# Attention's last four heads with the queries on partitions, divided and finished 128 tokens at a time

## The chip, the cores and the metric

The kernel runs on one core of a Trainium2 chip. What counts is the device time of one execution in microseconds. Three runs of the kernel before took 2172.04, 2159.49 and 2159.13 us (median 2159.49). A further execution under the hardware profiler gave the trace that all profile lines come from.

## The reference, cut to what matters

Two blocks of a model, each with a mixing layer and a mixture of experts side by side, on 8 sequences ("batches") of 512 tokens and 256 features. The change lies at the very end of the second block's attention:

```python
def _reference_tuple_inner(x, Wq, Wk, Wv, Wo, W_down_kv, W_up_k, W_up_v):
    ...
    scores = jnp.einsum('bhqd,bhkd->bhqk', qh, kh) * scale
    ...                                       # clip, decay by distance, clip
    attn = jax.nn.softmax(scores, axis=-1)
    out = jnp.einsum('bhqk,bhkd->bhqd', attn, vh)
    out = out.transpose(0, 2, 1, 3).reshape(B, S, D_MODEL)
    return (out @ Wo, latent_kv)
...
x = x + _L1_attn_ref(...) + _L1_ffn_ref(...)   # attention plus routed experts
```

There are 16 heads of 16 features. The softmax's division may come after the product with the values: the kernel keeps unnormalised exponentials, and each head's values carry a seventeenth column of ones, so that the product brings the sum of the exponentials along.

## The kernel before, in words

Everything is float32. The attention of the second block is a sequence of 128 steps, one for each batch b (8), group g of four heads (4) and chunk c of 128 queries (4). The order on every engine is the order in which the Python text issues instructions (a manual schedule); nothing is moved later. A loop over n = 0 to 130 issues step n's scores, step n-1's exponentials and step n-2's transposes in one pass, so three steps are in work at once.

- `Step.scores`: four matmuls (L1343) give 128 queries by 512 keys for four heads, in four PSUM banks. VectorE (DVE) clips them (L1348), multiplies by the decay and takes the maximum (L1350), and negates it (`ng`, L1354).
- `Step.exps`: ScalarE (ACT) takes exp with that maximum as bias (L1358).
- `Step.transpose`: TensorE (PE) turns each head's 128x512 exponentials, 128 columns at a time (L1365), into one of two banks `p_ps`; ACT copies them to `pT` (L1366), which holds keys on partitions and two chunks of queries as columns.
- `Step.values`: every second step, for a pair of chunks, 16 matmuls (L1374) with the values as stationary operand. `o_ps`, one bank, holds the four heads at partitions 0, 32, 64 and 96: 16 rows of output and the row of sums each, queries as columns.
- `divide`: a generator for each group, in the list `chains`, of which each pass of the loop runs one part. ACT copies `o_ps` to `os` (L1384), SP stores it to the DRAM tile `od` (L1385). In the next pass, after every second group (g = 1 and g = 3), the outputs come back as 128 rows of `oT` and the sums as a 128x32 tile `sm` (L1395, L1396); then DVE takes the reciprocal (L1401), SP stores it to `rd` and reads it back spread over each head's 16 rows as `rb` (L1402, L1404), and two passes later DVE multiplies (L1407). `oT` has two halves, [:, 0, :] for heads 0 to 7 and [:, 1, :] for heads 8 to 15.
- `finish`: for each 128 tokens two matmuls with `w_o` (L1287) into the one bank `bank`, an ACT copy `fo` (L1289), and DVE's addition to `x_sb` (L1291). Then `send` stores the batch's four tiles of 128 tokens (L1299).
- `combine` runs beside it: GpSimd (POOL) gathers the two expert rows of each token (L1308), and DVE adds them to `x_sb` (L1322), seven tiles behind; the last 14 additions are issued together in the last step with scores.

After the loop, what is left of `chains` and `finish` runs to its end. SP's queue holds all stores and loads named here, in the order of issue; one that waits holds up those behind it.

Of the kernel before, what the change touches and what calls it, by code (L numbers as in the profile page):

```python
# [8 lines left out]
FP = mybir.dt.float32  # L9
I32 = mybir.dt.int32  # L10
AF = mybir.ActivationFunctionType
ALU = mybir.AluOpType
# [4 lines left out]
P = 128  # L17
B, S, DM = 8, 512, 256
NT = B * S
NTILE = NT // P  # L20
TPB = S // P
KC = DM // P
# [18 lines left out]
AH, AD, DL = 16, 16, 64  # L41
# [9 lines left out]
def bc(ap, axis, shape):  # L51

    return ap.unsqueeze(axis).to_broadcast(shape)
# [3 lines left out]
def tile_kernel(ctx: ExitStack, tc: tile.TileContext, t, out: bass.AP):  # L57
    nc = tc.nc
    V, A, G, T, Y = nc.vector, nc.scalar, nc.gpsimd, nc.tensor, nc.sync
# [4 lines left out]
    def ctile(name, shape, dtype=FP, pool=None):  # L64
        return (pool or const).tile(shape, dtype, name=name, tag=name)
# [7 lines left out]
    ident = ctile("ident", [P, P])  # L73
# [238 lines left out]
    for d in range(2):  # L312
        for q in range(2):
            r = slice(q * HP2, (q + 1) * HP2)
# [19 lines left out]
    def bank(name, shape, tag="gen"):  # L334
        return mp.tile(shape, FP, name=name, tag=("e", "s")[tag] if isinstance(tag, int) else tag, bufs=2)
# [130 lines left out]
    with ExitStack() as es:  # L466
        p1, p2, psum = m1, m2, mp
# [490 lines left out]
        N = len(chunk)  # L958
# [37 lines left out]
        with tc.manual_schedule(engines=ENGINES):  # L996
# [34 lines left out]
            def fill(n):  # L1031
                for _ in range(n):
                    if next(rows, "end") == "end":
                        next(rest, None)
# [72 lines left out]
    x_sb = res.tile([P, NTILE, DM], FP, name="x_sb", tag="x_sb")  # L1107
    with tc.tile_pool(name="a1", bufs=1) as p1, tc.tile_pool(name="a2", bufs=2) as p2, tc.tile_pool(
        name="ap", bufs=1, space=PSUM
# [127 lines left out]
        def load_some(k):  # L1237
            for to, of in loads[:k]:
                Y.dma_start(out=to, in_=of)
            del loads[:k]  # L1240

        def inputs_of(b, xT, got):
            rows = rows_qk()
            got["v"] = p2.tile([P, TPB, VW], FP, name="vt", tag="vt")
            yield from project(
                xT, lat, lambda n: p1.tile([P, KC, S], FP, name=n + "c", tag="qkc"), got["v"], rows, bank,
                lambda n: spread(rows, got, n),
            )
# [28 lines left out]
        def turn(pool, i):  # L1277
# [2 lines left out]
            V.tensor_copy(at, slot1[:, i, :])  # L1280
            return at

        def finish(b, oT):
            for c in range(TPB):
                fp = bank("fin", [P, DM])
                for j in range(KC):
                    T.matmul(fp, oT[:, j, c * P : (c + 1) * P], w_o[:, j, :], start=(j == 0), stop=(j == KC - 1))  # L1287
                fo = p2.tile([P, DM], FP, name="fo", tag="fo")
                A.copy(fo, fp)  # L1289
                xi = x_sb[:, b * TPB + c, :]  # L1290
                V.tensor_tensor(xi, xi, fo, ALU.add)  # L1291
                yield
            finished.add(b)
            if b in combined:
                send(b)

        def send(b):
            for i in range(b * TPB, (b + 1) * TPB):
                Y.dma_start(out=out[i * P : (i + 1) * P, :], in_=x_sb[:, i, :])  # L1299
# [19 lines left out]
        def add(i, yg):  # L1319
            xi = x_sb[:, i, :]  # L1320
            for k in range(2):
                V.scalar_tensor_tensor(xi, yg[k], wsel[k][:, i : i + 1], xi, ALU.mult, ALU.add)  # L1322
            b = i // TPB
            if i % TPB == TPB - 1:
                combined.add(b)
                if b in finished:
                    send(b)

# [49 lines left out]
        def divide(b, g, op, od, rd, held):  # L1380


            os = p1.tile([P, S], FP, name="os", tag="row", bufs=2)
            A.copy(os, op)  # L1384
            Y.dma_start(out=od[g].rearrange("i r s -> (i r) s"), in_=os)  # L1385
            yield
            if g % 2 == 0:
                return
            j = g // 2
            if j == 0:  # L1390
                held.append(p1.tile([P, KC, S], FP, name="oT", tag="oT"))
            oT = held[0]
            sm = p2.tile([P, 32], FP, name="sm", tag="sm")
            for gg in range(2):
                Y.dma_start(out=oT[64 * gg : 64 * gg + 64, j, :], in_=od[2 * j + gg, :, :AD, :])  # L1395
                Y.dma_start(  # L1396
                    out=sm[64 * gg : 64 * gg + 64, :],
                    in_=od[2 * j + gg, :, AD, :].rearrange("i (p f) -> i p f", f=32),
                )
            yield  # L1400
            V.reciprocal(sm, sm)  # L1401
            Y.dma_start(out=rd[8 * j : 8 * j + 8, :].rearrange("h (p f) -> (h p) f", f=32), in_=sm)  # L1402
            rb = p1.tile([P, S], FP, name="rb", tag="row", bufs=2)
            Y.dma_start(out=rb, in_=bc(rd[8 * j : 8 * j + 8, :], 1, [8, AD, S]))  # L1404
            yield
            yield
            V.tensor_tensor(oT[:, j, :], oT[:, j, :], rb, ALU.mult)  # L1407
            yield
            if g == 3:
                urgent.insert(0, finish(b, oT))  # L1410
# [4 lines left out]
        with tc.manual_schedule(engines=ENGINES):  # L1415
# [3 lines left out]
            finished, combined = set(), set()  # L1419
            urgent, idle, chains = [], [], []  # L1420
# [26 lines left out]
            def more():  # L1447
                if ready is not None and n > ready + 3:
                    next(rows, None)
# [19 lines left out]
            N = len(steps)  # L1469
            last_rows(1)  # L1470
            done = []
            pT, op, pair = {}, {}, None
            inputs = {0: got}
            for n in range(N + 3):

                if n < N:
                    b, g, c = steps[n]
                    if (g, c) == (0, 3) and b + 1 < B:
                        xT = p2.tile([P, KC, S], FP, name="xT", tag="xT")
                        Y.dma_start(out=xT, in_=xtd1[b + 1])  # L1480
                    if (g, c) == (1, 2) and b + 1 < B:
                        inputs[b + 1] = {"q": [], "k": []}
                        urgent.append(inputs_of(b + 1, xT, inputs[b + 1]))
                    if (g, c) == (0, 0):
                        od = dram.tile([4, 4, 32, S], FP, name="od", tag="od", bufs=2)
                        rd = dram.tile([AH, S], FP, name="rd", tag="rd", bufs=2)
                        scratch = (od, rd, [])
                    now = Step(b, g, c, inputs[b])
                    now.scratch = scratch
                    done.append(now)  # L1490
                    now.scores()
                load_some(6)
                for chain in list(chains):
                    if next(chain, "end") == "end":
                        chains.remove(chain)
                if ready is not None and n == ready + 3:
                    idle.append(work)
                begun = n >= 1
                if begun:
                    fill()  # L1500
                if 1 <= n <= N:
                    done[n - 1].exps((0, 1))
                m = n - 2
                if m >= 0 and m % 2 == 0 and m >= 2:

                    s = done[m - 1]
                    if s.c == 1:
                        s_op = psum.tile([P, S], FP, name="o_ps", tag="o_ps", bufs=1)
                    s.values(s_pT, s_op)
                    if s.c == TPB - 1:  # L1510
                        chains.append(divide(s.b, s.g, s_op, *s.scratch))
                        next(chains[-1])
                    if begun:
                        fill()
                if 0 <= m < N:
                    if m % 2 == 0:
                        s_pT = [p2.tile([P, TPB, 2 * P], FP, name="pT", tag="pT", bufs=5) for _ in range(4)]
                    done[m].transpose(s_pT, (0, 1))
                if begun:
                    fill() or more()  # L1520
                if 1 <= n <= N:
                    done[n - 1].exps((2,))
                if 0 <= m < N:
                    done[m].transpose(s_pT, (2,))
                    if m % 2 == 1 and n < N // 2:
                        fill()
                    done[m].transpose(s_pT, (3,))
                if begun:
                    fill() or more()
                if 1 <= n <= N:  # L1530
                    done[n - 1].exps((3,))
                follow()
# [80 lines left out]
```

## Time and profile before

| | |
|---|---|
| median of three runs | 2159.49 us (2159.13 to 2172.04) |
| the profiled execution's own time | 2153.93 us |
| its span in the trace | 2152.2 us |
| mean granted TensorE clock | 0.929 |
| PE, DVE, ACT, POOL busy | 1874.2, 1463.6, 1187.6, 636.4 us |
| last maxima of the scores done on DVE | 2117.07 us |
| last group's values end on PE | 2125.9 us |
| last group's product with the reciprocals begins on DVE | 2138.87 us |
| last addition to `x_sb` | 2148.88 us, 0.42 us long |

Times in the trace are microseconds from the start of the span. A line of an engine's timeline gives the start, the duration of the run of equal instructions, the engine, the source line, the operation with its output and inputs, their sizes, how many, and in brackets the idle time before it and what ended it. A float32 matmul of the program shows as two records on PE. PEld is the loading of the stationary operand, SPq is SP's queue. In a line of the windows stand the stretch and its length, the busy time and number of instructions of PE, PEld, DVE, ACT and POOL, then the granted TensorE clock (1.00 is full speed), the share of the DMA engines, and GB/s.

### The profile page before, as it was taken

How to read it: one execution, taken by the hardware profiler on the slowest of the kernel's cores; microseconds unless marked ns; L12 is line 12 of the kernel's file. 1: busy time of each engine (PE TensorE's matmuls, PEld its weight loads, DVE VectorE, ACT ScalarE, POOL GpSimd, SP SyncE). 2: the span in 40 equal slices, each digit the busy share in tenths (PEclk: the TensorE clock that was granted, in tenths of full speed). 3: DMA queues.
4: the chain of work that ended last, by engine and by line, in shares of the span. 5: the costliest groups of instructions: out<-in, count | busy, mean ns of one | idle time of the engine just before them, and what ended most of it. 6: DMA issues, size and time to landing. Idle time of an engine off the chain costs nothing. (4 is left out here: it accounts for less than half of the span.)

```text
span 2152.2 us, 33599 instructions
## 1 busy us (share of the span) xinstructions
PE 1874.2 (87%) x11792; PEld 1240.4 (58%) x11792; DVE 1463.6 (68%) x3328; ACT 1187.6 (55%) x2562; POOL 636.4 (30%) x592
## 2 busy tenths in 40 slices
PE   5649999999999999987867778999999999999785
PEld 5325666766766676644544444656666666666343
DVE  5745666767584666577648896766666676767795
ACT  2235453545444354545426676767677777777563
POOL 0075453646363454445410253000000000000452
PEclk9879999999999999988887788999999999999787
DMA  7134454646463464444523342121121212121354
GB/s 257 56 103 169 152 191 146 222 142 221 140 203 138 135 230 134 142 135 127 162 94 112 96 144 89 63 103 61 65 81 60 97 63 82 62 77 54 89 109 94
DMA packets 156361, 263.69 MB, mean 123 GB/s; under 512 B 25018, under 2 KB 112622, under 8 KB 144290
## 3 DMA queue, kind: packets, MB, share of 16 engines
q1 hardware_dynamic: 124544, 144.70, 21.2%
q0 software_dynamic: 22320, 107.55, 15.3%
q10 hardware_dynamic: 9330, 9.31, 1.3%
q8 instruction: 93, 1.52, 0.3%
q14 instruction: 74, 0.61, 0.1%
HBM read 193.44 MB, written 72.75 MB: 124 GB/s over the span
## 5 line engine op out<-in xcount | busy, mean ns | idle before, releaser
L1348 DVE TENSOR_SCALAR s<-s_ps 128x512 f32<-128x512 f32 x512 | 317.7, 683 | 235.8 <-PE s_ps L1343 185.9
L1358 ACT ACTIVATE s<-s,ng 128x512 f32<-128x512 f32 x512 | 354.2, 726 | 29.0 <-DVE ng L1354 22.2
L1365 PE MATMUL p_ps<-ident,s 128*128 128x128 f32 x2048 | 297.3, 289 | 71.0 <-ACT pT L1366 60.2
L1365 PEld LDWEIGHTS p_ps<-ident,s 128*128 128x128 f32 x2048 | 244.3, 147 | 155.9 <-ACT pT L1366 94.2
L1366 ACT COPY pT<-p_ps 128x512 f32<-128x512 f32 x512 | 278.9, 590 | 88.5 <-PE p_ps L1365 63.9
L1350 DVE CUSTOM_DVE_ANT_0 s<-s,band 128x512 f32<-128x512 f32 x512 | 322.5, 685 | 0.0
L1308 POOL DMA_INDIRECT yg<-yd,at x64 | 67.6, 1057 | 710.6 <-PE s_ps L1343 650.7
L688 PE MATMUL pj<-xT,w_in 128*128 128x512 f32 x384 | 197.5, 640 | 12.3 <-DVE cv L701 9.5
L1343 PE MATMUL s_ps<-kT,qT 16*128 16x512 f32 x1024 | 174.7, 698 | 17.5 <-DVE s L1348 10.9
L507 PEld LDWEIGHTS h_ps<-xdT,w 128*128 128x128 f32 x1248 | 153.9, 197 | 32.9 <-issue 19.0
L507 PE MATMUL h_ps<-xdT,w 128*128 128x128 f32 x1248 | 158.8, 282 | 10.3 <-ACT xdT L497 10.3
L864 POOL TENSOR_TENSOR au<-da,half 128x512 f32<-128x512 f32 x64 | 75.1, 1174 | 258.0 <-PE seg L879 162.4
L701 DVE SCALAR_TENSOR_TENSOR cv<-pj,w_conv_w,cv 128x511 f32<-128x511 f32 (+2 forms) x192 | 143.0, 746 | 9.8 <-issue 5.6
L520 PE MATMUL y_ps<-w,hT 128*128 128x256 f32 x624 | 148.2, 380 | 0.0
L1374 PE MATMUL o_ps<-pT,vt 128*32 128x256 f32 x2048 | 139.6, 415 | 0.0
L520 PEld LDWEIGHTS y_ps<-w,hT 128*128 128x128 f32 x624 | 115.9, 191 | 34.8 <-issue 19.4
L937 POOL TENSOR_TENSOR yT<-yT,ex 128x512 f32<-128x512 f32 (+1 forms) x48 | 59.9, 1248 | 255.7 <-DVE ex L936 193.6
L1200 PE MATMUL e_hp<-e_xdT,e_w 128*128 128x256 f32 x448 | 121.7, 394 | 3.0 <-ACT e_xdT L1194 2.0
L688 PEld LDWEIGHTS pj<-xT,w_in 128*128 128x128 f32 x384 | 70.6, 201 | 91.9 <-issue 82.5
L926 DVE TENSOR_TENSOR yT<-yT,yd 128x512 f32<-128x512 f32 (+1 forms) x64 | 43.8, 684 | 116.4 <-PE yd L917 114.3
L1213 PE MATMUL e_yp<-e_w,e_hT 128*128 128x256 f32 x448 | 120.0, 390 | 0.2
L1374 PEld LDWEIGHTS o_ps<-pT,vt 128*32 128x32 f32 x2048 | 64.5, 118 | 80.0 <-issue 51.1
(275 smaller groups left out, 3133.1 us busy)
## 6 DMA issues: line engine op xcount, KB each, us to landing
ex<-exd SPq DMA_DIRECT2D x96, 128.0 KB
u<-in_u_dram SPq DMA_DIRECT2D x16, 512.0 KB
xtd<-xT SPq DMA_DIRECT2D x16, 512.0 KB
fr<-fdd SPq DMA_DIRECT2D x64, 128.0 KB
od<-os SPq DMA_DIRECT2D x32, 256.0 KB
xT<-xtd SPq DMA_DIRECT2D x15, 512.0 KB
e_w<-in_ei_dram SPq DMA_DIRECT2D x7, 1024.0 KB
e_w<-in_eo_dram SPq DMA_DIRECT2D x7, 1024.0 KB
```

The costliest lines, as they stand in the source:

```text
L507: T.matmul(hp[:, i, :], w1[:, k * FF + f * P : k * FF + (f + 1) * P], xdT[:, k * P : (k + 1) * P], start=(k == 0), stop=(k == KC - 1),)
L520: T.matmul(yp, hT[f // 4][:, f % 4, :], w2[:, f * DM : (f + 1) * DM], start=(f == 0), stop=(f == FC - 1))
L688: T.matmul(pj, w_in[:, k, o * P : (o + 1) * P], self.xT[:, k, :], start=(k == 0), stop=(k == KC - 1))
L701: V.scalar_tensor_tensor(cv[:, s:], pj[:, : S - s], conv_w[:, q, 3 - s : 4 - s], cv[:, s:], ALU.mult, ALU.add)
L1200: T.matmul(hp, w1[:, k, f * P : (f + 1) * P], xdT[:, k, :], start=(k == 0), stop=(k == KC - 1))
L1343: T.matmul(sp[i], self.q[r, cols], self.k[r, :], start=True, stop=True)
L1348: V.tensor_scalar(self.p[i], sp[i], -CLAMP, CLAMP, ALU.max, ALU.min)
L1350: V.tensor_tensor_reduce(out=self.p[i], in0=self.p[i], in1=band[:, at : at + S], scale=1.0, scalar=-3.0e38, op0=ALU.mult, op1=ALU.max, acc ...
L1358: A.activation(self.p[i], self.p[i], AF.Exp, bias=self.ng[:, i : i + 1])
L1365: T.transpose(pp[:, k, :], self.p[i][:, k * P : (k + 1) * P], ident)
L1366: A.copy(pT[i][:, :, cc * P : (cc + 1) * P], pp)
L1374: T.matmul(op[32 * i : 32 * i + 32, half * 2 * P : (half + 1) * 2 * P], self.v[:, k, h * (AD + 1) : h * (AD + 1) + 32], pT[i][:, k, :], st ...
```

## The change

Only batch 7 and its last group (heads 12 to 15) are affected. There, in place of `values` for pairs of chunks, each chunk gets a generator `last_group` as soon as its transposes are done: 16 matmuls with 128 queries of `pT` as stationary operand and 17 columns of values as moving operand give queries on partitions; DVE takes the reciprocal of the four columns of sums and multiplies. In the next pass a matmul with the identity turns the 128x64 result into partitions 64 to 127, and ACT copies it into `oT`'s upper half. Then, once heads 8 to 11 are divided, two matmuls with `w_o` follow, DVE adds their result from PSUM to `x_sb`, and the tile is sent by itself. `o_q` and `t_q` use the one bank of `o_ps`.

Heads 8 to 11 (g = 2) can no longer wait for g = 3: `divide` treats them alone (`ending`), on 64 rows, and tells `last_group` by a second entry in `held`.

```diff
+        def last_group(s, held):
+            op = psum.tile([P, 4, AD + 1], FP, name="o_q", tag="o_ps", bufs=1)
+            cols = slice(s.c % 2 * P, (s.c % 2 + 1) * P)
+            for i in range(4):
+                h = 4 * s.g + i
+                for k in range(TPB):
+                    T.matmul(
+                        op[:, i, :], s.pT[i][:, k, cols], s.v[:, k, h * (AD + 1) : (h + 1) * (AD + 1)],
+                        start=(k == 0), stop=(k == TPB - 1),
+                    )
+            sm = p2.tile([P, 4], FP, name="smq", tag="smq")
+            V.reciprocal(sm, op[:, :, AD])
+            oq = p2.tile([P, 4, AD], FP, name="oq", tag="oq")
+            V.tensor_tensor(oq, op[:, :, :AD], bc(sm, 2, [P, 4, AD]), ALU.mult)
+            yield
+            oT = held[0]
+            qs = slice(s.c * P, (s.c + 1) * P)
+            tp = psum.tile([P, P], FP, name="t_q", tag="o_ps", bufs=1)
+            T.matmul(tp[64:, :], oq.rearrange("p i d -> p (i d)"), ident, start=True, stop=True)
+            A.copy(oT[64:, 1, qs], tp[64:, :])
+            yield
+            while not held[1:]:
+                yield
+            fp = bank("fin", [P, DM])
+            for j in range(KC):
+                T.matmul(fp, oT[:, j, qs], w_o[:, j, :], start=(j == 0), stop=(j == KC - 1))
+            i = s.b * TPB + s.c
+            V.tensor_tensor(x_sb[:, i, :], x_sb[:, i, :], fp, ALU.add)
+            last_sent.add(s.c)
+            if s.b in combined:
+                send_tile(i)
...
@@ add
                 if b in finished:
                     send(b)
+                elif b == B - 1:
+                    for c in last_sent:
+                        send_tile(b * TPB + c)
...
@@ divide
-            if g % 2 == 0:
+            ending = b == B - 1 and g == 2
+            if g % 2 == 0 and not ending:
                 return
...
-            for gg in range(2):
+            r, nh = (slice(0, 64), 4) if ending else (slice(0, P), 8)
+            for gg in range(nh // 4):
                 Y.dma_start(out=oT[64 * gg : 64 * gg + 64, j, :], in_=od[2 * j + gg, :, :AD, :])
...
-            V.tensor_tensor(oT[:, j, :], oT[:, j, :], rb, ALU.mult)
+            V.tensor_tensor(oT[r, j, :], oT[r, j, :], rb[r], ALU.mult)
+            if ending:
+                held.append(True)
...
@@ the loop over n
-                if m >= 0 and m % 2 == 0 and m >= 2:
+                if m > N - TPB:
+                    chains.append(last_group(done[m - 1], done[m - 1].scratch[2]))
+                    next(chains[-1])
+                elif m >= 0 and m % 2 == 0 and m >= 2:
...
+                    done[m].pT = s_pT
```

In the changed program the instructions of every engine stand in the same order as before up to the scores of the very last step; from there on they differ. On SP the loads of heads 8 to 11 stand between batch 5's and batch 6's stores, and their `rd` and `rb` behind batch 6's.

More of the change, by code (lines that the diff above doesn't have):

```diff
@@ L1281, in turn, with send_tile @@
             return at
+        def last_group(s, held):
[29 more added lines that the diff above has]
+                send_tile(i)
+        last_sent = set()
+        def send_tile(i):
+            Y.dma_start(out=out[i * P : (i + 1) * P, :], in_=x_sb[:, i, :])
         def finish(b, oT):
@@ L1400, in divide @@
             yield
-            V.reciprocal(sm, sm)
-            Y.dma_start(out=rd[8 * j : 8 * j + 8, :].rearrange("h (p f) -> (h p) f", f=32), in_=sm)
+            V.reciprocal(sm[r], sm[r])
+            Y.dma_start(out=rd[8 * j : 8 * j + nh, :].rearrange("h (p f) -> (h p) f", f=32), in_=sm[r])
             rb = p1.tile([P, S], FP, name="rb", tag="row", bufs=2)
-            Y.dma_start(out=rb, in_=bc(rd[8 * j : 8 * j + 8, :], 1, [8, AD, S]))
+            Y.dma_start(out=rb[r], in_=bc(rd[8 * j : 8 * j + nh, :], 1, [nh, AD, S]))
             yield
             yield
-            V.tensor_tensor(oT[:, j, :], oT[:, j, :], rb, ALU.mult)
+            V.tensor_tensor(oT[r, j, :], oT[r, j, :], rb[r], ALU.mult)
+            if ending:
+                held.append(True)
             yield
```

## The prediction

> **What bounds the kernel now.** I read the page, then the chain of waits that ended last, then each engine's timeline from 2085 us on, because the change touches nothing earlier: engine by engine, both kernels issue the same instructions up to the last four heads of batch 7. Chunk c below is that group's 128 queries c = 0 to 3. The end of the chain, with its columns start us, us, what:
>
> ```profile
> 2122.13 1.14 PE p_ps L1365 x8
> 2123.27 2.61 PE o_ps L1374 x32
> ...
> 2126.51 2.00 DMA od<-os
> ...
> 2129.08 4.11 DMA sm<-od
> ...
> 2135.09 3.66 DMA rb<-rd
> ...
> 2146.37 2.09 PE fin L1287 x4
> ...
> 2148.88 0.42 DVE x_sb L1291
> ```
>
> After the last transposes and values come 13 us of copies through DRAM in which the engines hardly work, then four output products one after the other, the last three at some 2.09 us. The same four records at 2055 us, in PE's timeline:
>
> ```profile
> 2055.68 1.03 PE L1287 MATMUL fin<-w_w_o,oT 128*128 128x256 f32 x4
> ...
> 2062.50 1.93 PE L1374 MATMUL o_ps<-pT,vt 128*32 128x256 f32 x32
> ```
>
> The windows say why; the column after the engines is the granted clock. It goes to 0.50 at 2129, after the wait began, and stays there while fin runs. So the end is a chain of latencies at half clock, and before 2117.1 DVE sets the pace (it ends chunk 3's maxima at 2117.07 and has no gap before).
>
> ```profile
> 2126.00:2128.00 2.00, 0.49 (x2) 0.09 (x1) 0.00 (x0) 0.49 (x1) 0.00 (x0) 1.00 0.33 124
> 2128.00:2130.00 2.00, 0.00 (x0) 0.00 (x0) 0.00 (x0) 0.00 (x0) 0.00 (x0) 0.74 0.23 68
> 2140.00:2142.00 2.00, 1.54 (x4) 0.73 (x4) 0.43 (x1) 0.37 (x1) 0.00 (x0) 0.50 0.00 0
> ```
>
> **What goes.** For this group: two values() calls (32 records each, 2.91 us at 2114.01 and 2.66 us at 2123.20), the os copy, od store, four loads, reciprocal, rd and rb, and four fo copies on ACT. The round trip through DRAM does not vanish: heads 8 to 11 still make it, one step earlier and with half the rows.
>
> **What comes.** For each chunk: 16 small matmuls (Q0 to Q3), two small DVE operations, one turning matmul (R0 to R3), one ACT copy, then fin (F0 to F3). PE's new order is: scores of chunk 3, Q0, transposes of chunk 1, R0, Q1, transposes of 2, R1, Q2, transposes of 3, F0, F1, R2, Q3, F2, R3, F3. Q and R share the single o_ps bank, so Q of the next chunk waits until ACT has copied R.
>
> The price of Q decides. The nearest row has the same full 128x128 stationary operand and few moving columns: 8 at line 603, 24 at line 148, where Q moves 17.
>
> ```profile
> 69.08 3.67 PE L148 MATMUL pp<-w_w_small,xT 128*128 128x24 f32 x16 [0.51 <-ACT xT L144]
> ...
> 959.21 1.85 PE L603 MATMUL pp<-w_w_r,xT 128*128 128x8 f32 x16
> ...
> 1061.12 3.65 PE L603 MATMUL pp<-w_w_r,xT 128*128 128x8 f32 x16 [0.18 <-ACT xT L597]
> ```
>
> The program's 8 matmuls are 16 records, so Q is 32 records. Full clock: (1.85 - 0.25 for the last) / 15 = 0.107 us apart, and 31 x 0.107 + 0.25 = 3.57 us. Half clock: (3.65 - 0.38) / 15 = 0.218, so 7.14 us. Three times as many columns (line 148) change nothing, so the weight loads set it. Bounds per Q at full clock: 1.93 us from line 1374 above (weights of 32 columns) and 31 x 0.121 + 0.29 = 4.0 us from line 1365 (1.14 us for 8, 128 columns moving). I take line 603, the nearest.
>
> The other rows: the 128x4 reciprocal 0.17 (L165), the 128x64 product 0.22 (between 0.187 for 128x32 at L608 and 0.257 for 128x96 at L152), together 0.39; R 0.4 (two 128x128 records, 0.39 at L900, 0.64 at half clock); the 64x128 ACT copy 0.3 (0.37 for 128x256 at L1289); transposes of two heads 1.1 (half clock 1.94 to 2.18); pT copies 1.06 a pair; exponentials 0.65 each; fin 1.05, or 2.07; its addition 0.42; handovers 0.05.
>
> **The sum at full clock**, from 2117.07, which both kernels share. Q0 runs 2110.4 to 2113.9 under DVE's maxima and costs nothing there; it and chunk 1's transposes push ACT to 2117.9, eating the 1.53 us that ACT waited at 2117.1. Without DVE's cover Q0 would add its 3.57. DVE's 0.39 stands ahead of the 14 additions of expert rows (6.50 us). R0 ends 2117.95 and the copy 2118.25. Behind it on ACT wait chunk 3's exponentials (1.15 us late), behind R0 on PE wait Q1 and chunk 2's transposes, which feed ACT in turn. Q1 ends 2121.85. Chunk 2's transposes and copies and chunk 3's last exponential end on ACT at 2125.85. DVE has done its additions at 2123.96, the reciprocal of heads 8 to 11 at 2124.3, chunk 1's division at 2124.7; R1 is ready, its copy ends 2126.15. Q2 ends 2129.75, chunk 3's transposes 2132.05.
>
> Heads 8 to 11: SP now issues their loads after batch 5's four stores and ahead of batch 6's (before, all eight stood together, 2107.45 to 2120.17). Batch 5's last addition is at 2110.9, so the loads land near 2116.5, before DVE asks. rd stands behind batch 6's stores, whose last addition is at 2120.3, also done by 2124.3. From the reciprocal's end to the product took 2133.64 to 2138.87, 5.23 us; here it gives 2129.55, and DVE's product ends 2130.85. This lies 1.2 us under chunk 3's transposes.
>
> F0 ends 2133.1, its addition 2133.55, F1 2134.65, R2 2135.05, copy 2135.4, Q3 2138.95, F2 2140.0, R3 2140.4, copy 2140.7. F3's first half waits for F2's addition (one bank) and it ends 2141.5, addition 2141.95. From the last addition to the end of the span, 2149.30 to 2152.2, are 2.9 us: 2144.85, or 7.3 us less than 2152.2.
>
> **But the clock.** A full clock has to survive the Qs. Line 603 ran from 1044.93 to 1046.66 (14 records), begun at full clock; the windows there:
>
> ```profile
> 1045.00:1046.00 1.00, 1.00 (x10) 1.00 (x10) 1.00 (x1) 0.00 (x0) 0.00 (x0) 1.00 0.30 123
> 1046.00:1047.00 1.00, 1.00 (x8) 0.87 (x10) 0.40 (x3) 0.00 (x0) 0.00 (x0) 0.98 1.08 352
> 1047.00:1048.00 1.00, 1.00 (x4) 0.00 (x0) 0.93 (x4) 0.00 (x0) 0.00 (x0) 0.50 0.85 226
> ```
>
> PE was recorded busy through 1045 to 1047 and the clock fell all the same. The records at 1061 and 69 us ran at half and did not raise it either. Steady transposes do: 16 records from 1155.37 at half clock, and at 1159.6 it is full. Falls and rises at 2084.6, 2091.4, 2098.2, 2105.1 and 2129.0 stand apart by multiples of about 3.4 us. A Q lasts about as long as one such interval, so I expect Q1, Q2 and Q3 at half clock and the transposes and fins mostly at full. Each Q then costs 3.57 more, all in series: 3 x 3.57 = 10.7, so 2155.55, or 3.4 us more than before. **This is the forecast**: the profiled execution took 2153.93 us with a span of 2152.2, the median of the runs shown is 2159.49, and I put the difference on the median: 2162.9.
>
> [...]
>
> **Rivals.** *The clock holds* (2152.2, 7.3 us faster). For it: between 2105 and 2128 the clock is 1.00 with PE busy some 60 to 100%, and records at 959 us ended at full. Against it: 1047 us, and a Q is twice as long as those.
>
> *All of it at half clock* (slower). Place: from about 2118, when PE has waited for R0. Working on from Q1 at 2118.25 with 7.14 per Q, 4.05 for a chunk's transposes, 2.07 per fin and 0.65 per R: Q1 2125.4, ACT free 2130.6, Q2 2138.05, transposes 2142.1, F0 2144.2, F1 2146.7, Q3 2154.85, F2 2156.9, F3 2159.6, addition 2160.05, end 2162.95. That is 10.8 us slower, 2170.3. It decides if no interval after 2118 is filled well enough to raise the clock; for it speaks that fin at 2140 to 2150 never did. With the upper bound for Q at half clock (8.0), 2.6 more.
>
> *The round trip decides* (Q near its lower bound, 1.93). F0 then waits for DVE's product near 2130.1, and the rest with a short Q3 ends 2140.65: 11.5 us faster, 2148.0. Against it: no row with 128-column weights is that quick.
>
> *The change does not shorten the chain*, because heads 8 to 11 come late: the loads would have to land after 2124, 8 us later than worked out, and chunk 1's division would stand behind them on DVE at a microsecond per microsecond. The od store is issued at 2107.08 and took 2.00 us in the chain, so I see no cause.
>
> **How the numbers follow.** Qs at half and the rest at full 0.45; clock holds 0.25; all at half 0.2; round trip 0.05; something else 0.05. No case reaches 1% (21.6 us, about what a measurement of this kernel can tell from no change), so nearly all the chance is on no change. The forecast's own range is one Q either way at the other clock, 2159.3 to 2166.5. The whole range runs from the full-clock sum on the profiled execution's own time (2153.93 - 7.3 = 2146.6) to the all-half sum with a dear Q on the median, 2172.
>
> **What would show it.** Right: 32-record rows of o_q near 7.1 us for Q1 to Q3 and 3.6 for Q0; granted clock 0.50 in windows inside the Qs; chain through o_q, t_q, oT and fin without DMA after the last transposes; a last addition near 2152. Rows of o_q at 3.6 throughout mean that the clock held; fin at 2.07 after 2132 means all at half. A DMA rb or sm row at the end of the chain, or any change before 2110, would make the reasoning wrong.

## The result, and the profile after

The changed kernel takes 2165.43 us, the median of 20 runs (2153.08 to 2174.64); the kernel before, beside it, 2161.53 us (20 runs, 2152.76 to 2173.29). The ratio, which goes by the means and not by the medians, is 1.001 with a 95% interval of 0.9992 to 1.0028: +2.2 us, between -1.7 and +6.0. That is no change, as forecast; the forecast's +3.4 us is a ratio of 1.0016, inside the interval.

The profiled execution has a span of 2160.2 us against 2152.2, 8.0 us more. 5.6 of these lie ahead of the tail: chunk 3's maxima end on DVE at 2122.67 here and at 2117.07 before, and both kernels issue the same instructions in the same order up to there on DVE, on PE up to the last scores. Over the twelve traces of this study of which this holds, this end lay anywhere from 2107.7 to 2128.6. So I read every trace from there. The **tail**, from the end of the last maxima to the end of the span, is 35.13 us before and 37.53 after.

PE's timeline of the tail, as before:

```profile
2113.48 3.75 PE L1291 MATMUL o_q<-vt,pT 128*128 128x17 f32 x32
2117.07 3.65 PE L1407 MATMUL p_ps<-ident,s 128*128 128x128 f32 x16
2123.06 0.43 PE L1303 MATMUL t_q<-ident,oq 128*64 128x128 f32 x2 [2.34 <-DVE oq L1298]
2123.84 6.90 PE L1291 MATMUL o_q<-vt,pT 128*128 128x17 f32 x32 [0.35 <-ACT oT L1304]
2130.58 3.79 PE L1407 MATMUL p_ps<-ident,s 128*128 128x128 f32 x16
2134.30 0.43 PE L1303 MATMUL t_q<-ident,oq 128*64 128x128 f32 x2
2136.01 5.54 PE L1291 MATMUL o_q<-vt,pT 128*128 128x17 f32 x32 [1.27 <-ACT oT L1304]
2141.38 3.49 PE L1407 MATMUL p_ps<-ident,s 128*128 128x128 f32 x16
2144.71 1.03 PE L1310 MATMUL fin<-w_w_o,oT 128*128 128x256 f32 x4
2146.25 1.13 PE L1310 MATMUL fin<-w_w_o,oT 128*128 128x256 f32 x4 [0.52 <-DVE x_sb L1312]
...
2148.09 4.11 PE L1291 MATMUL o_q<-vt,pT 128*128 128x17 f32 x32 [0.35 <-ACT oT L1304]
2152.04 2.05 PE L1310 MATMUL fin<-w_w_o,oT 128*128 128x256 f32 x4
2154.03 0.69 PE L1303 MATMUL t_q<-ident,oq 128*64 128x128 f32 x2
2154.65 2.08 PE L1310 MATMUL fin<-w_w_o,oT 128*128 128x256 f32 x4
```

Where the kernel before had 13 us of copies through DRAM, PE now has work nearly all the time, and none of it is quick. The four Qs are the rows of o_q: 3.75, 6.90, 5.54 and 4.11 us. The windows over them (window, its length, busy us of PE, PEld, DVE, ACT, POOL, then the granted clock, third from the end):

```profile
2116.00:2118.00 2.00, 2.00 (x16) 2.00 (x17) 1.93 (x7) 0.39 (x1) 1.00 (x1) 0.79 0.88 110
...
2136.00:2138.00 2.00, 1.99 (x17) 1.99 (x17) 0.00 (x0) 0.00 (x0) 0.00 (x0) 0.91 0.00 0
2138.00:2140.00 2.00, 2.00 (x11) 2.00 (x11) 0.00 (x0) 0.00 (x0) 0.00 (x0) 0.50 0.00 0
...
2146.00:2148.00 2.00, 1.49 (x6) 0.87 (x6) 0.62 (x2) 0.22 (x1) 0.00 (x0) 1.00 0.20 66
...
2152.00:2154.00 2.00, 2.00 (x5) 1.20 (x5) 0.41 (x2) 0.00 (x0) 0.00 (x0) 0.50 0.00 0
```

Windows of 1 us put the falls near 2117.2, 2124.0, 2137.7 and 2151.3, one in or just before each Q, and the rises near 2120.6, 2134.2 and 2144.5: neighbours stand about 3.4, 6.8 or 10.2 us apart. At 2117 and 2151 the 3.4 us before the fall hold nothing but Q0 and Q3, with PE recorded busy all along (but for 0.2 us of waiting at 2148). The fall at 2137.7 comes after R1, 1.27 us of waiting and 1.7 us of Q2 (17 records in 2136 to 2138, then 11), and the one at 2124 after a wait, R0's 2.34 us for DVE (PE was busy for 0.72 us of the 3.4 before it). The chunk's transposes that follow a Q begin at half, and under each of them the clock rises again (near 2120.6, 2134.2 and 2144.5). The end of the chain (start us, us, what) has no DMA row from 2117 on, and from the end of the maxima at 2122.67 on it runs through PE but for small steps of ACT and DVE, 0.62 us at most:

```profile
2136.01 5.54 PE o_q L1291 x32
2141.55 3.33 PE p_ps L1407 x16
2144.87 0.88 PE fin L1310 x4
...
2148.09 4.11 PE o_q L1291 x32
2152.20 1.89 PE fin L1310 x4
...
2154.72 2.02 PE fin L1310 x4
```

### The profile page after: what moved, and what is told of

The parts are those of the page before. It is cut to its first block, busy times and chain, and to the rows that moved or that the text cites. A ratio compares the mean times of both kernels' runs of the same rounds, so it can differ in the third digit from the quotient of the medians.

```text
span 2160.2 us, 33744 instructions
## 1 busy us (share of the span) xinstructions
PE 1896.2 (88%) x11864; PEld 1262.0 (58%) x11864; DVE 1464.5 (68%) x3336; ACT 1187.8 (55%) x2561; POOL 637.7 (30%) x592
## 5 line engine op out<-in xcount | busy, mean ns | idle before, releaser
L1407 PE MATMUL p_ps<-ident,s 128*128 128x128 f32 x2048 | 305.9, 295 | 63.9 <-ACT pT L1408 46.4
L1407 PEld LDWEIGHTS p_ps<-ident,s 128*128 128x128 f32 x2048 | 252.5, 151 | 149.9 <-ACT pT L1408 74.9
L1416 PE MATMUL o_ps<-pT,vt 128*32 128x256 f32 x1984 | 132.8, 413 | 0.0
L892 ACT ACTIVATE mt<-seg,mid 64x64 f32<-64x64 f32 x512 | 109.5, 308 | 0.8
```

Source lines behind the costliest of these rows:

```text
L1407: T.transpose(pp[:, k, :], self.p[i][:, k * P : (k + 1) * P], ident)
L1416: T.matmul(op[32 * i : 32 * i + 32, half * 2 * P : (half + 1) * 2 * P], self.v[:, k, h * (AD + 1) : h * (AD + 1) + 32], pT[i][:, k, :], st ...
```

## The experiments

The theory: the changed kernel's tail is a chain on PE, and its length is set by the clock, which falls in the Qs because records with 17 moving columns do not count as work for it. Rivals: the clock falls because of the waits around the Qs (PE idle 0.35 to 2.34 us before R and Q, since o_q and t_q share a bank); or the Qs are slow for another reason, such as their weight loads, whatever the clock; or the clock has nothing to do with the moving columns, and any back-to-back stream holds it. Full clock for the same chain was worked out in the prediction as a tail of 27.8 us (2144.85 - 2117.07).

**q128: Qs with 128 moving columns.** The same 32 records and weights, 111 more columns that nobody uses.

```diff
-            op = psum.tile([P, 4, AD + 1], FP, name="o_q", tag="o_ps", bufs=1)
+            op = psum.tile([P, 4, 128], FP, name="o_q", tag="o_ps", bufs=1)
...
-                        op[:, i, :], s.pT[i][:, k, cols], s.v[:, k, h * (AD + 1) : (h + 1) * (AD + 1)],
+                        op[:, i, :], s.pT[i][:, k, cols], s.v[:, k, h * (AD + 1) - 95 : h * (AD + 1) - 95 + 128],
...
-            V.reciprocal(sm, op[:, :, AD])
+            V.reciprocal(sm, op[:, :, 95 + AD])
...
-            V.tensor_tensor(oq, op[:, :, :AD], bc(sm, 2, [P, 4, AD]), ALU.mult)
+            V.tensor_tensor(oq, op[:, :, 95 : 95 + AD], bc(sm, 2, [P, 4, AD]), ALU.mult)
```

> Only the moving operand of the small matmuls is widened from 17 to 128 columns of the values (the other 111 columns are computed and not used). The tail is counted from the end of the last maxima on DVE to the end of the span: 35.1 us before, 37.5 us after. Theory (a stream of narrow matmuls lets the clock fall, though PE's records are back to back): wider ones hold it at 1.00, each group of 32 records takes about 4.0 us (31 x 0.121 + 0.29) in place of 6.90, 5.54 and 4.11, fins take 1.05, and the tail is the full-clock sum 27.8 + 3 x 0.43 = 29.1 us, some 8 us shorter than after. Rival (PE's waits for DVE and ACT let it fall): the clock falls just the same, the groups take 4 to 8 us and the tail is 37.5 us or more.

Measured: the tail is 31.60 us, between the theory's 29.1 and the rival's 37.5. Over 12 runs the median is 2150.23 against 2155.81 before beside it, the ratio 0.9993 (0.9969 to 1.0017). So more arithmetic makes the tail 5.9 us shorter than the changed kernel's 37.53, and the whole is still not measurably different from before. Q2 took 5.35 us. PE's timeline, Q1 with what is ahead of it, then Q3, and two windows:

```profile
2115.99 0.68 PE L1303 MATMUL t_q<-ident,oq 128*64 128x128 f32 x2 [1.34 <-DVE oq L1298]
2117.03 4.98 PE L1291 MATMUL o_q<-vt,pT 128*128 128x128 f32 x32 [0.35 <-ACT oT L1304]
...
2137.31 3.84 PE L1291 MATMUL o_q<-vt,pT 128*128 128x128 f32 x32 [0.35 <-ACT oT L1304]
```

```profile
2117.00:2119.00 2.00, 1.97 (x9) 1.98 (x10) 1.93 (x5) 1.33 (x2) 0.00 (x0) 0.50 0.95 90
2119.00:2121.00 2.00, 2.00 (x18) 2.00 (x18) 1.89 (x6) 0.00 (x0) 0.00 (x0) 0.89 0.90 106
```

At full clock 128 columns cost as much as 17 (3.84 against 3.75 us), so the moving columns are not what a Q's time goes into. The theory alone does not stand, though: the clock still fell twice, near 2116.0 and 2126.3, when in the 3.4 us before PE had been busy for 1.35 and 1.59 us only (waits of 1.34 and 1.38 us for DVE ahead of R, and shorter ones between the transposes). What differs is that it rose again inside the Q, near 2119.5, when of the 3.4 us before 2.4 were Q1, 0.68 R0 and the rest a wait. (The clock also rises within a Q of 17 columns, at 2130 in own_bank_2 below, but there after 3.4 us that were nearly all transposes and R0.) Waits and thin records both let it fall.

**q68: 68 moving columns**, the same edit with 51 for 95 and 68 for 128.

> The same with 68 columns. The weight loads (0.107 us apart) still set the pace at full clock, so a group costs 3.6 us if the clock holds; the columns stream for about half of the time that they do with 128. Theory: a tail between 27.8 us (the clock holds) and 37.5 us (it falls as with 17), which tells how wide is wide enough; I expect it nearer to 28 to 32. Rival (PE's waits): 37.5 us, as with 17 columns.

Measured: tail 35.76 us, a miss (28 to 32 was expected), one run of 2159.35 beside 2155.81. Q0 is 5.64 us, Q1 5.89; Q2, and Q3 with F2 behind it:

```profile
2133.88 6.41 PE L1291 MATMUL o_q<-vt,pT 128*128 128x68 f32 x32 [1.47 <-ACT oT L1304]
...
2147.62 3.79 PE L1291 MATMUL o_q<-vt,pT 128*128 128x68 f32 x32 [0.35 <-ACT oT L1304]
2151.25 1.08 PE L1310 MATMUL fin<-w_w_o,oT 128*128 128x256 f32 x4
```

The windows give the clock 0.66 in 2134 to 2136 and 0.50 from there to 2144, past Q2's end at 2140.3. So half the columns of q128 did not bring it back in Q2, and Q3 began and ended at full. Q3 did that with 17 columns in other traces too (own_bank, after_3 below), but there the clock fell right behind it: F2 took 1.65 to 2.05 us in all five traces with 17 columns, and here 1.08 us, with the windows at 1.00 from 2146 to 2152. In this one trace 68 columns did not raise a fallen clock, yet they held a full one through Q3; the tail is nearer to that with 17 than to that with 128.

**own_bank: t_q in a bank of its own**, so that Q does not wait for ACT's copy of R.

```diff
-            tp = psum.tile([P, P], FP, name="t_q", tag="o_ps", bufs=1)
-            T.matmul(tp[64:, :], oq.rearrange("p i d -> p (i d)"), ident, start=True, stop=True)
-            A.copy(oT[64:, 1, qs], tp[64:, :])
+            tp = psum.tile([P, S], FP, name="t_q", tag="s_ps", bufs=4)
+            T.matmul(tp[64:, :P], oq.rearrange("p i d -> p (i d)"), ident, start=True, stop=True)
+            A.copy(oT[64:, 1, qs], tp[64:, :P])
```

> The turned result t_q goes to a bank of the scores, free by then, so the next chunk's small matmuls no longer wait until ACT has copied it. Theory (the clock is what was lost): only the idle time of PE ahead of the three groups goes, 0.35 + 1.27 + 0.35 = 2.0 us, so a tail of about 35.5 us, give or take 2 for where the clock's intervals fall; the groups still take 4 to 7 us. Rival (the one bank shared by o_q and t_q is what was lost): most of the 9.7 us above the full-clock sum come back, a tail near 28 us.

Measured: tail 32.78 us, a miss (less than expected), one run of 2143.96 beside 2155.81. Q1 and Q2 in PE's timeline, with no idle time noted before them; Q3 took 3.75:

```profile
2110.08 6.48 PE L1291 MATMUL o_q<-vt,pT 128*128 128x17 f32 x32
...
2120.74 3.91 PE L1291 MATMUL o_q<-vt,pT 128*128 128x17 f32 x32
```

The waits gone are worth 0.35 + 1.27 + 0.35 = 1.97 us; the rest of the 4.75 us against the changed kernel is clock. The edit does not touch the Qs, and yet Q1 to Q3 take 14.14 us instead of 16.55, F2 and F3 3.58 instead of 4.13. Whether that follows from the edit or from luck was the next question.

**own_bank_2, after_2, after_3: the same kernels again.**

> The bank of its own for the turned result with 17 columns, once more: its tail was 32.8 us where 35.5 was expected, with two groups at 3.9 and 3.75 us. Theory: 2 us are the waits taken out, the rest was where the intervals fell, so now a tail of 31 to 37 us with other groups slow. Rival (the shared bank is worth nearly 5 us of itself): 32 to 33 us again with the same groups fast.

> The changed kernel once more, for how far its tail of 37.5 us goes from one execution to the next. Theory: the clock's intervals of some 3.4 us fall elsewhere against the groups each time, so each group lies between 3.6 and 7 us and the tail between 33 and 39 us; Q0 at full clock or fallen within, at least two of the four groups at over 4.5 us.

> The same a third time: a tail between 33 and 39 us, and at least two of the four groups at over 4.5 us.

Measured, one run each (2165.03, 2161.4 and 2149.18 us, beside 2153.46 before):

| trace | Q0 | Q1 | Q2 | Q3 | tail |
|---|---|---|---|---|---|
| after | 3.75 | 6.90 | 5.54 | 4.11 | 37.53 |
| after_2 | 3.79 | 7.01 | 5.66 | 4.23 | 37.65 |
| after_3 | 6.59 | 4.87 | 4.77 | 3.75 | 36.07 |
| own_bank | 3.75 | 6.48 | 3.91 | 3.75 | 32.78 |
| own_bank_2 | 6.45 | 3.90 | 4.44 | 5.74 | 34.48 |

From PE's timeline of after_3, Q0, then Q3 with F2:

```profile
2102.04 6.59 PE L1291 MATMUL o_q<-vt,pT 128*128 128x17 f32 x32
...
2136.05 3.75 PE L1291 MATMUL o_q<-vt,pT 128*128 128x17 f32 x32 [0.35 <-ACT oT L1304]
2139.64 1.65 PE L1310 MATMUL fin<-w_w_o,oT 128*128 128x256 f32 x4
```

All three tails lie where they were expected, and own_bank_2 does not repeat own_bank's fast groups. The same program can give each Q another time: it depends on where the falls and rises of the clock happen to lie against it (in after the clock fell near the end of Q0, in after_3 near 2102.5, 0.5 us after its start). One pair of traces is therefore good to a few microseconds only. The changed kernel's tail is 36.1 to 37.7, mean 37.1; own_bank's mean 33.6, some 3.5 us less, of which 1.97 are the waits. The rest (1.5 us on two traces) I would not build on.

**before_warm and before_warm2: the kernel before with PE kept busy.** During its copies through DRAM, 12 tiles (25 in the second) of four transposes whose result nobody reads.

```diff
@@ ahead of the last fill() in the kernel before
+            for _ in range(25):
+                warm = psum.tile([P, TPB, P], FP, name="warm", tag="p_ps", bufs=2)
+                for k in range(TPB):
+                    T.transpose(warm[:, k, :], ident, ident)
```

> The kernel before with 48 transposes of the identity on PE after the last values, some 11.6 us that lie in the wait for the copies through DRAM; their results are not used. Theory: the granted clock stays at 1.00, fin takes 1.05 us in place of 2.09, and the tail of 35.1 us shrinks by about 3.6 us to 31.5. Rival (fin is slow at the end for another reason, such as its single bank): 35.1 us.

> As before_warm, but with 100 transposes: there each took one record and not two, so 48 of them filled only 5.5 us and the clock fell before fin came. 100 last about 11.6 us, to some 1 us ahead of fin. Theory: granted clock 1.00 until fin, fin at 1.05 us, tail 35.1 - 3.6 = 31.5 us. Rival: fin slow for another reason, 35 us.

The first missed its purpose, because I had sized it wrongly: a transpose is one record and not two, as a matmul is. Its tail is 36.02 us (2153.47 beside 2155.81), the second's 31.64 (2141.07 beside 2151.76). The rows of the filler and the second output product, first of before_warm:

```profile
2124.50 5.46 PE L1536 MATMUL warm<-ident 128*128 128x128 f32 x48
...
2140.86 2.07 PE L1287 MATMUL fin<-w_w_o,oT 128*128 128x256 f32 x4 [0.46 <-ACT fo L1289]
```

Then of before_warm2, whose granted clock is 1.00 in every window from 2116 to 2132:

```profile
2116.38 11.14 PE L1536 MATMUL warm<-ident 128*128 128x128 f32 x100
...
2131.25 1.13 PE L1287 MATMUL fin<-w_w_o,oT 128*128 128x256 f32 x4 [0.46 <-ACT fo L1289]
```

With 11 us of filler the clock lives to the end and fin takes 1.13 instead of 2.07 us; the tail is 3.5 us shorter than before's 35.13, as expected. With 5.5 us it falls near 2134, before fin. With nothing but the filler changed this gives the price of the clock in that tail, and shows that transposes hold it; it is one trace of each.

**before_thin: the same place, Q-like records instead.** 8 tiles of four matmuls with 17 moving columns.

```diff
+            for _ in range(8):
+                thin = psum.tile([P, TPB, P], FP, name="thin", tag="p_ps", bufs=2)
+                for k in range(TPB):
+                    T.matmul(thin[:, k, : AD + 1], s_pT[0][:, k, :P], done[-1].v[:, k, : AD + 1], start=True, stop=True)
```

> The same place filled with 32 matmuls as the change has them, full 128x128 weights and 17 moving columns (64 records, nothing waits between them, results not used). Theory (narrow ones do not count as work for the clock): PE is recorded busy without a gap, yet the clock goes to 0.50 within 3.4 to 7 us of their start, and the records' distance doubles from 0.107 to 0.218 us, so that they last 8 to 12 us and not 6.9. Rival (only waits let it fall): 1.00 throughout, 6.9 us.

Measured: tail 34.89 us, one run of 2153.64 beside 2151.76. PE's timeline and the windows; fin takes 2.07 us after it:

```profile
2125.73 11.24 PE L1536 MATMUL thin<-vt,pT 128*128 128x17 f32 x64
```

```profile
2125.00:2127.00 2.00, 2.00 (x22) 1.48 (x14) 0.00 (x0) 0.58 (x1) 0.00 (x0) 1.00 0.00 0
2127.00:2129.00 2.00, 2.00 (x19) 2.00 (x18) 0.00 (x0) 0.00 (x0) 0.00 (x0) 0.90 0.46 146
2129.00:2131.00 2.00, 2.00 (x11) 2.00 (x11) 0.00 (x0) 0.00 (x0) 0.00 (x0) 0.50 0.25 76
```

64 records without a gap, with PE recorded busy for 2.00 of 2.00 us, and the clock falls from 1.00 to 0.50 about 3 us after their start and stays. At full clock they would have taken 64 x 0.107 = 6.9 us. No wait plays a part. This shows the step that decided the forecast: records with so few moving columns do not hold the clock, though PE is recorded busy. The rival that any back-to-back stream holds it falls.

**q128_own: both edits, wide Qs and t_q in its own bank.**

> The changed kernel with both edits, 128 moving columns and a bank of its own for the turned result. With 128 columns the clock still fell twice, each time after PE had waited 1.4 + 0.35 us for DVE and for the copy. Theory (both the narrow streams and the waits between them let it fall): with both gone or shortened the groups take 3.8 to 4.5 us and the tail comes to 28 to 31 us. Rival (it falls on where the intervals lie, and neither edit matters): 31 to 37 us.

Measured: tail 26.45 us, less than the 28 to 31 expected, one run of 2137.3 beside 2151.76. All four Qs took 3.84 us, and the granted clock is 1.00 from Q0 to F3. Q2:

```profile
2116.68 3.84 PE L1291 MATMUL o_q<-vt,pT 128*128 128x128 f32 x32
```

Without thin records and without the waits for the bank the clock holds (PE's longest wait from Q0 on is 1.20 us, within chunk 1's transposes), and the full-clock sum of the prediction comes near: 27.8 us. Cut at the ends of R0, Q1, Q2, F0, Q3 and the last addition, six of its seven stretches come within 0.25 us; the one from Q1's to Q2's end took 6.87 us instead of 7.90, and in it lay the wait for the bank that this kernel does not have. It is one trace; the rival, by which only the place of the clock's intervals matters, expected 31 us or more. By this trace, thin records and the waits were what stood between the changed kernel and the gain at full clock.

**turn_all: another way to the same end.** The kernel before, with heads 8 to 15 kept out of DRAM without turning the product round: `values` stays as it was (32 stationary columns, 256 moving), its result is copied to SBUF, 128x128 transposes bring queries onto partitions, DVE divides by columns, and matmuls with the identity turn it back. The fins alternate between two banks, and DVE adds straight from PSUM.

```diff
+        def turned(os, cols, tag):
+            tp = psum.tile([P, TPB, P], FP, name="t_" + tag, ...)
+            for k, c in enumerate(cols):
+                T.transpose(tp[:, k, :], os[:, c * P : (c + 1) * P], ident)
...
+            for k in range(n):
+                V.reciprocal(sm[:, k, :], t4[:, k, :, AD])
+                V.tensor_tensor(
+                    oq[:, k, :].rearrange("p (i d) -> p i d", d=AD), t4[:, k, :, :AD],
+                    bc(sm[:, k, :], 2, [P, 4, AD]), ALU.mult,
+                )
...
+        def into(oT, oq, cols, r):
+            tq = psum.tile([P, S], FP, name="t_o", tag="s_ps", bufs=4)
+            for k, c in enumerate(cols):
+                T.matmul(tq[r, k * P : (k + 1) * P], oq[:, k, :], ident, start=True, stop=True)
+            A.copy(oT[r, 1, cols[0] * P : (cols[-1] + 1) * P], tq[r, : len(cols) * P])
...
+            for c in range(TPB):
+                fp = psum.tile([P, DM], FP, name="fin", tag="p_ps", bufs=2)
...
+                V.tensor_tensor(x_sb[:, i, :], x_sb[:, i, :], fp, ALU.add)
```

> A kernel of its own, from the one before: the last group's values stay as they were (weights of 32 columns), but the output is turned on PE to 128 queries on partitions (one transpose for a chunk), divided by columns, turned back with a matmul, and the fins run in two banks with one store each; heads 8 to 11 of batch 7 go the same way, so no copy through DRAM is left after them. Theory (narrow matmuls with 128 weight columns were what cost, the idea of dividing by columns was sound): no group of 3.6 to 7 us is left, values end some 7 us after the last maxima, then 10 us of short steps and 2.9 us to the end of the span: a tail of 19 to 23 us against 35.1 before and 37.5 after, 12 to 16 us or 0.6 to 0.75% faster than before. Rival (a chain of short steps loses as much in handovers and at half clock): 30 us or more, no difference in the runs.

Measured: tail 18.50 us, just under the 19 to 23 expected; 2134.69 us median of 9 runs against 2151.76 (14 runs) beside it, ratio 0.9928 (0.9903 to 0.9954). That is 0.7% faster than the kernel before, clear of the noise, and its interval lies wholly below the changed kernel's. Several things changed at once here, so no single one of them has a price from this run. PE's timeline of its end, and a window:

```profile
2116.35 1.93 PE L1374 MATMUL o_last<-pT,vt 128*32 128x256 f32 x32
2118.21 1.00 PE L1385 MATMUL t_g<-ident,os 128*128 128x128 f32 x4
2119.28 1.38 PE L1401 MATMUL t_o<-ident,oq 128*64 128x128 f32 x8
2120.59 3.72 PE L1592 MATMUL fin<-w_w_o,oT 128*128 128x256 f32 x16
```

```profile
2121.00:2123.00 2.00, 2.00 (x11) 1.76 (x10) 0.80 (x2) 0.06 (x1) 0.00 (x0) 1.00 0.00 0
```

The product for two chunks takes 1.93 us here, where two Qs take 7.5 at full clock. The clock is 1.00 to the end, and the 16 records of the four output products take 3.72 us.

## Why the prediction was right

The forecast was no change, by a full-clock gain of 7.3 us that the clock takes back with 10.7. The measured +2.2 us (-1.7 to +6.0), and the tails of 37.1 after against 35.3 before (means of three traces each, that of the kernel before over its own, before_warm and before_thin, whose fillers did not change fin's time), +1.7, say the same; +3.4 was forecast. That the verdict is no change says little by itself, since the prediction's own cases, from 11.5 us faster to 10.8 us slower, all lie under its 1%. The interval says more: it leaves out the rivals at -11.5, -7.3 and +10.8 us. The rival in which the clock holds (27.8 us of tail) is refuted by the traces, and q128_own shows what would have made it true. In the all-half rival F0 and F1 take 2.07 us; they take 1.03 and 1.13. The round trip does not decide: DVE's timeline has heads 8 to 11 ready before F0 starts at 2144.71.

```profile
2122.57 0.17 DVE L1296 RECIPROCAL smq<-o_q 128x4 f32<-128x4 f32 x1
2122.78 0.22 DVE L1298 TENSOR_TENSOR oq<-o_q,smq 128x64 f32<-128x64 f32 x1
...
2129.34 0.34 DVE L1445 RECIPROCAL sm<-sm 64x32 f32<-64x32 f32 x1
2130.78 0.18 DVE L1296 RECIPROCAL smq<-o_q 128x4 f32<-128x4 f32 x1 [1.11 <-PE o_q L1291]
...
2141.94 0.67 DVE L1451 TENSOR_TENSOR oT<-oT,rb 64x512 f32<-64x512 f32 x1
```

They also show the loads of heads 8 to 11 hidden, since L1445 waits for nothing, and chunk 1's division waiting for PE rather than for DVE. The durations of 0.17 and 0.22 are the ones the prediction took, and R's 0.43 on PE is close to its 0.4; a Q at full clock took 3.75 us, 0.18 more than its 3.57.

The sum, stretch by stretch from the end of the last maxima:

| stretch | forecast | measured |
|---|---|---|
| to R0's end | 0.88 | 0.82 |
| to Q1's end | 7.47 | 7.25 |
| to Q2's end | 11.47 | 10.81 |
| to F0's end | 3.35 | 4.19 |
| to Q3's end | 9.42 | 6.46 |
| to the last addition's end | 3.00 | 4.98 |
| to the end of the span | 2.90 | 3.02 |

It ends within 1 us, 38.5 against 37.5, partly by **errors that cancel**. The step that failed is "Q1, Q2 and Q3 at half clock and the transposes and fins mostly at full". The clock follows with a lag (the transposes behind Q1 begin at 2130.58, and it rises near 2134.2): Q1, Q2 and Q3 took 6.90, 5.54 and 4.11 us (16.55) in place of 21.4, since Q2 and Q3 begin at the full clock that the transposes before them raised (Q1 had 0.2 us of it); in return the transposes behind Q1 and Q2 run at half for a while (3.79 and 3.49 us instead of about 2.2), and F2 and F3 take 2.05 and 2.08 in place of 1.05. Half clock thus fell on other instructions than I gave it to, in about the right amount: 22.5 us from the last maxima to F3's end, where three Qs at 7.14 make 21.4. That the amounts agree is partly luck, as the traces differ. The clock also fell at the end of Q0 (near 2117), which cost nothing, as forecast for Q0 as a whole: R0 waited 2.34 us for DVE afterwards. In after_3, where nearly all of Q0 ran at half (6.59 us), R0 had no such wait, so that cover is used up there.

A second term was missing as a cause: the waits. The forecast blamed the thin records alone; only its all-half rival let the clock fall at PE's wait for R0. There it did fall, at 2124, ahead of nearly all of Q1; q128 falls after waits of 1.34 and 1.38 us, and in q128_own, with wide Qs and no wait over 1.20 us, no fall is left.

Two workings of the prediction are off, and neither moves the forecast. It took the records at 69 us for half clock; that follows from their spacing alone, since the windows there read 1.00. What it drew from them, that more columns cost no time, q128 shows directly (3.84 against 3.75 us). And by its own terms the round-trip rival ends near 2141.3 and not at 2140.65, and the whole range at 2172.8 and not at 2172.

What stays open: why the end of the last maxima moves by 21 us between executions of the same instructions. The mean granted clock goes along with the span (0.921 at 2163.1, 0.941 at 2139.3), which fits but proves nothing. Also what exactly lowers and raises the clock: 17 columns let the clock fall, 128 held and raised it, and 68 did some of each in one trace.

## What to carry to other kernels

Before turning a product round, count its records and look at what each moves: 128 stationary columns with 17 moving ones cost here nearly four times as much PE time at full clock as 32 with 256 (7.5 against 1.93 us for two chunks), and they let the clock fall (from 1.00 to 0.50 in before_thin), which the work behind them pays for as well (F2 and F3 of the changed kernel took 2.05 and 2.08 us, F0 and F1 1.03 and 1.13). When a wait on a DMA is replaced by a chain on one engine, price that chain at the clock that it will itself bring about. And a stage whose clock falls in an unavoidable wait (at 2129 in the kernel before) can be worth filling with work that holds it, as 100 transposes did here (1.00 throughout): that alone took 3.5 us off the tail of the kernel before, in one trace.

## What the runs showed of the hardware

- A PE recorded busy does not by itself keep the clock: 64 fp32 records of 128x128 weights and 17 moving columns, back to back, let the granted clock fall from 1.00 to 0.50 within about 3 us; 100 transposes of 128x128 in the same place held 1.00 for 11.14 us.
- Moving 128 columns instead of 17 is all but free in such records (3.84 against 3.75 us for 32 at full clock). With 128 columns and a bank of its own for the turned result the clock stayed at 1.00 in one trace, where with 17 it fell to 0.50 in both; with 128 and the shared bank it fell twice, to 0.50.
- A fp32 matmul leaves two records on PE, a transpose one: 48 transposes were 48 records in 5.46 us, 32 matmuls were 64.
- The same program's tail differs by 1.6 us between its traces, in which the clock falls at other places: 36.07, 37.53 and 37.65 us.
